# Spreading a layernorm's deviations over the partitions by selecting products, in the tail and for the first band

## The chip, the cores and the metric

The kernel runs on one core of one Trainium2 chip. The metric is the device time of an execution in microseconds (us); the median of several runs is given. The core has five engines that work side by side: TensorE (PE, with its weight loads PEld), VectorE (DVE), ScalarE (ACT), GpSimd (POOL) and SyncE (SP), and 16 DMA engines that all of them share. Here SP issues most transfers, ACT and POOL a few.

## The reference

The input x is (4, 128, 128, 128): four images of 128 channels and 128 x 128 pixels, float32. First comes a block with regional attention and a depthwise convolution, then two quantised 3x3 convolutions:

```python
reg = x[:, :, ih, iw]                      # regions of 16 x 16, step 14: 9 x 9 of them an image
tok = reg...reshape(b * n, rs * rs, c)
y = _ln(tok, ln1_g, ln1_b)                 # layernorm over the 128 channels
qkv = y @ w_qkv                            # 4 heads of 32
tok = softmax(q @ k.T * hd**-0.5) @ v @ w_out + b_out + tok
merged = out / cnt                         # regions added up where they overlap
y = _ln(xf, ln2_g, ln2_b) @ w_p0 + b_p0    # xf: merged, 128 channels; y: 256 channels
ym = depthwise 5x5 convolution of y
ym = gelu(batchnorm(ym)); y = gelu(ym) @ w_p2 + b_p2 + xf
...
# then: clip, 4-bit quantise, conv3x3, batchnorm, relu, quantise, conv3x3, batchnorm, add the identity
```

`_ln` takes the mean and the variance of a pixel over its 128 channels, and multiplies the centred pixel by one number, the inverse deviation `rsqrt(v + eps)`. This number is what the change is about.

## The kernel before

Channels lie on the 128 partitions and pixels along the free axis, so the sums of a layernorm run over partitions. The kernel doesn't centre: the weights that follow are multiplied by a centring matrix once, at the start. It needs only the inverse deviation of every pixel, on every partition.

The work goes by bands. A band is 16 rows of an image, the step is 14, so an image has NR = 9 bands and the four have T = 36. A band is cut into two blocks of up to LB = 8 rows, that is 1024 pixels. For each block `normalise` makes five steps:

- `squares`: ACT squares the block.
- `variance`: eight products on PE, with a column block of ones, 32 wide. The pixels are taken in four quarters of w = n / 4 = 256; the sums of quarter q are written to the 32 partitions from 32 q on, so each number stands on 32 partitions. ACT and DVE make the variance from two such sums (L364 to L368).
- `deviation`: ACT takes logarithm and exponential (L372, L373), which gives the tile `rstd` (128 x 256). Then ACT's queue stores one partition in 32 of it, four rows of 256, to a small tensor `row` in DRAM (L375).
- `spread`: SP's queue loads `row` back into a tile `xn` (128 x 1024), the four rows side by side, the same on all 128 partitions (L380).
- `scaled`: DVE multiplies the block by it in two halves, in place in `xn` (L389).

`ln1_chunks` uses this for the first layernorm, with the projections to queries and keys after it (L459, results copied by ACT); `post_chunks` for the second, with the products by w_out ahead of it (L511, L512) and the projection to 256 channels after it (`p0`, L527; ACT adds the bias, L532, and SP stores y to `y2_d` in DRAM). All products go through one pool of PSUM tiles, `pm`, with three buffers; the scores of the attention have their own.

The order of PE, ACT, DVE and SP is written out by hand, POOL's follows from the program too. For band 0 the first layernorm's steps run alone, the two blocks step by step (`for steps in zip(*ln1_chunks(0))`). Then, in every band t, `beside(t)` gives the work that is put between the nine regions' attention: the first layernorm of band t + 1, the second of band t - 1, steps of the depthwise convolution of an image that is done. There a row of deviations is on its way while PE works on attention.

After the last band comes a tail. The pools of the bands (`xp`, `yp`, `up`, `cp`, the attention's) are closed, and two pools `late1`, `late2` are opened on their memory. Then:

- `run(left)`: the last projections of the band before the last; SP stores them.
- `conv_rest`: allots the input tiles `u0` to `u7` and the weight tiles `w0` to `w7` of the last depthwise unit (rows 96 to 127 of the last image), issues all weight loads on POOL (L552, sixteen of 240 KB), and on SP the early part of the input loads of the first `early` tiles: rows that were stored before, of the first of two row groups (L655, two of 144 KB a tile).
- `run(beside(T))`: the second layernorm of the last band, alone. `row`, `xn`, `p0`, stores of y.
- `rest()`: the input loads that are left, `late(k)`, four of them ahead of the steps and then one with each step; and eight steps of the convolution, each with 96 small products (L566, 192 PE records), two copies by ACT (L686), statistics by DVE (L690), and stores of the result, half on SP's queue, half on ACT's (L695).

`late(k)` fetches, for a tile with an early part, the rest of the rows; for a tile without, the whole tile in four loads (two of 256 KB, two of 64 KB).

After the tail the batchnorm statistics are gathered, then follow the gelu stage and the two quantised convolutions; the change doesn't touch them. A second, safe form of the kernel's first half is built too and runs only when a flag says that scores may be large; it doesn't run with these inputs.

DMAs of SP and ACT take one of eight completion counters in turn, and a DMA waits until the last one on its counter has landed.

Of the kernel before, what the change touches and what calls it, by code (L numbers as in the profile page):

```python
# [22 lines left out]
LB = 8  # L23
# [23 lines left out]
def layers(  # L47
# [29 lines left out]
    nc = tc.nc  # L77
# [32 lines left out]
    ident = const.tile([P, P], F32, name="ident")  # L110
# [22 lines left out]
    with (  # L133
# [21 lines left out]
        for w in (wqkv, wp0.rearrange("p h m -> p (h m)")):  # L155
            n = w.shape[1]
# [18 lines left out]
    with ExitStack() as actx:  # L175
# [21 lines left out]
        xb, xr, yr, qs, kr, ob = {}, {}, {}, {}, {}, {}  # L197

        def scratch(n):

            return up.tile([P, 32 * CW], F32, name="u")[:, :n]
# [137 lines left out]

            return [load, largest, spread, clip_all, widen, to_int, to_f8]  # L340

        def normalise(src, n):

            held = {}
            w = n // 4

            def squares():  # L350
                held["sq"] = sq = work.tile([P, LB * P], F32, name="sq")
                nc.scalar.activation(sq[:, :n], src(), AF.Square)

            def variance():
                ps = ps_m.tile([P, 2, 256], F32, name="pm")
                for m, v in enumerate((src(), held.pop("sq"))):
                    for q in range(4):
                        nc.tensor.matmul(  # L358
                            ps[32 * q : 32 * q + 32, m, :w], ones, v[:, q * w : (q + 1) * w],
                            start=True, stop=True,  # L360
                        )
                held["rstd"] = rstd = dev.tile([P, 256], F32, name="rstd")
                rstd = rstd[:, :w]
                nc.scalar.activation(rstd, ps[:, 0, :w], AF.Square, scale=1.0 / P)  # L364
                nc.vector.scalar_tensor_tensor(
                    rstd, ps[:, 1, :w], 1.0 / P, rstd, ALU.mult, ALU.subtract
                )
                nc.vector.tensor_scalar(rstd, rstd, 0.0, None, ALU.max)  # L368

            def deviation():  # L370
                rstd = held.pop("rstd")[:, :w]
                nc.scalar.activation(rstd, rstd, AF.Ln, bias=eps_t)  # L372
                nc.scalar.activation(rstd, rstd, AF.Exp, scale=-0.5)  # L373
                held["row"] = row = rowp.tile([4, 256], F32, name="row")
                nc.scalar.dma_start(out=row[:, :w], in_=rstd[0:P:32, :])  # L375

            def spread():
                row = held.pop("row")
                held["xn"] = xn = xnp.tile([P, LB * P], F32, name="xn")
                nc.sync.dma_start(  # L380
                    out=xn[:, :n].rearrange("p (q w) -> p q w", q=4),
                    in_=bass.AP(row.tensor, row.offset, [[0, P], [256, 4], [1, w]]),
                )

            def scaled():
                xn = held.pop("xn")
                halves = [xn[:, hh * n // 2 : (hh + 1) * n // 2] for hh in range(2)]
                for hh, t in enumerate(halves):
                    nc.vector.tensor_tensor(t, t, src()[:, hh * n // 2 : (hh + 1) * n // 2], ALU.mult)  # L389
                return halves  # L390

            return squares, variance, deviation, spread, scaled
# [44 lines left out]
                        held[t][:, :, 0:2, :], held[t - 1][:, :, RS - 2 :, :]  # L437
                    )

        def ln1_chunks(t):  # L440

            chunks = []
            for at, (r, n) in enumerate(row_blocks(t)):
                held = {}
                squares, variance, deviation, spread, scaled = normalise(lambda r=r, n=n: xb[t, r][:, : n * P], n * P)

                def second(r=r, n=n, at=at, held=held, scaled=scaled):
                    held["xn"] = scaled()
# [42 lines left out]

            xr[t, n] = load_rows(rp, "xr", t, *finished(t)[n])

        def post_chunks(t):


            b, i = bands[t]
# [1 line left out]
            for at, (r, n) in enumerate(finished(t)):  # L499
                held = {}  # L500
                squares, variance, deviation, spread, scaled = normalise(
                    lambda n=n, held=held: held["xf"][:, : n * P], n * P
                )

                def project(hh, r=r, n=n, at=at, held=held):
# [138 lines left out]
        def conv_rest(n, w_t, u_t, c_t):  # L644
# [1 line left out]


            b, g0, ng = units[n]
            early = 5
            at = GR + 2  # L650

            def load(k, a, z, g, m):
# [193 lines left out]
        def beside(t):  # L846
# [5 lines left out]
            two = post_chunks(t - 1) if t else []  # L852
            had = len(todo)
            if t >= 2:
                b, i = bands[t - 2]
# [11 lines left out]
            n = len(todo) // share[0] if fresh else -(-len(todo) // max(share[0], 1))  # L867
# [63 lines left out]
        ga2, be2 = vector(gamma2, "ga2"), vector(beta2, "be2")  # L931
        with nullcontext() if safe else tc.manual_schedule(engines=MANUAL):
            ln1_begin(0)
            for steps in zip(*ln1_chunks(0)):
                run(steps)
            last = None
            for t in range(T):
# [88 lines left out]
    with (  # L1026
# [14 lines left out]
        for m in range(2):  # L1041
# [3 lines left out]
            for h in range(2):  # L1045
# [3 lines left out]
                    start=True, stop=True,  # L1049
# [301 lines left out]
```

## Time and profile before

| | us |
|---|---|
| median of 3 runs | 3292.92 |
| lowest, highest | 3278.27, 3293.81 |
| the profiled execution | 3289.4 |
| its span | 3287.5 |

| engine | busy us | share |
|---|---|---|
| PE | 3089.1 | 94% |
| DVE | 2018.0 | 61% |
| ACT | 1989.9 | 61% |
| POOL | 836.3 | 25% |

Where the stages lie in the profiled execution: the first layernorm of band 0 from 9 to 34 us, the bands from there to 2229, the tail from 2229 to 2334, then the gelu stage and the convolutions.

How to read the views. The timeline has, for each row, the start and the length in us, the engine (SPq, ACTq: that engine's queue issues a DMA), the line, the operation, what is written and read, how many instructions were merged, and in brackets how long the engine was idle before and what released it. The row of a DMA issue shows the issue alone, not the transfer. A float32 product of 128 x 512 is two PE records. The windows view has one row a stretch: its length, the busy time of PE, PEld, DVE, ACT and POOL (number of instructions), the granted clock of TensorE as a share of the full one, the share of the 16 DMA engines that was busy, and GB/s. The waits view has who waited for whom, us in total, times, and the longest. In the DMA view a queue has its packets, MB and share of the 16 engines' time; q1 is SP's queue, q10 ACT's, q0 POOL's. An issue row has the KB of one DMA and the median us to its landing.

### The profile page before, as it was taken

To read this page: it belongs to the slowest core of one execution; us is meant where nothing else is said; L and a number is where in the kernel's file an instruction comes from. 1 tells how busy PE (TensorE), PEld (TensorE's weight loads), DVE (VectorE), ACT (ScalarE), POOL (GpSimd) and SP (SyncE) were. 2 spreads that over 40 slices of the span, in tenths; PEclk is the share of its full clock that TensorE was granted. 3 is DMA by queue.
4 is the path that set the end of the run, shared out by engine and by line. 5 is a ranking of instruction groups with operands and counts; after the bars stand their busy time and mean duration, and the time that the engine had idled before them with its cause. 6 is when DMAs were issued, how large, how long until landed. Compare 5 with 4: busy or idle time off the path is not lost.

```text
span 3287.5 us, 75680 instructions
## 1 busy us (share of the span) xinstructions
PE 3089.1 (94%) x30922; PEld 1540.7 (47%) x30922; DVE 2018.0 (61%) x3247; ACT 1989.9 (61%) x2654; POOL 836.3 (25%) x1058
## 2 busy tenths in 40 slices
PE   7999999999999999999999998884899999999998
PEld 3555554544444554444444444553544444444343
DVE  4877887676766667666655564442455555666543
ACT  5777776777777776777656564432477767433443
POOL 3444443333333333333222232211111111000000
PEclk8999999999999999999999998876699999999999
DMA  4555677898886788886888888757899999452398
GB/s 92 133 164 166 173 181 177 195 212 196 204 202 163 192 208 204 195 208 166 190 200 207 202 195 201 192 160 186 256 356 358 358 358 300 150 167 70 101 359 308
DMA packets 810450, 682.75 MB, mean 208 GB/s; under 512 B 581014, under 2 KB 696047, under 8 KB 810095
## 3 DMA queue, kind: packets, MB, share of 16 engines
q1 hardware_dynamic: 799471, 671.26, 75.2%
q8 instruction: 246, 4.03, 0.5%
q0 software_dynamic: 1024, 3.93, 0.5%
q10 hardware_dynamic: 9600, 2.62, 0.4%
q14 instruction: 109, 0.89, 0.1%
HBM read 410.81 MB, written 270.81 MB: 207 GB/s over the span
## 4 chain that ended last, share of the span: by engine, by line
PE 76%; DMA 9%; ACT 5%; issue 4%; DVE 3%; SPq 2%; POOL 0%; ACTq 0%; DVEq 0%; POOLq 0%
PE pc L1125 19%; PE pm L566 9%; PE sc L749 9%; PE po L812 8%; PE pm L459 7%; PE pb L1183 6%; PE pm L527 5%; PE pm L735 4%; PE po L820 3%; DMA y_d<-y 3%; PE pm L358 3%; PE pm L511 3%; DMA u<-y_d 2%; ACT pt L757 1%; DMA xn<-row 1%
## 5 line engine op out<-in xcount | busy, mean ns | idle before, releaser
L832 DVE RECIPROCAL rd<-po 128x256 f32<-128x256 f32 x324 | 569.3, 1757 | 451.6 <-PE po L820 446.5
L1125 PE MATMUL pc<-q,wq 128*128 128x512 fp8e4 x3168 | 701.4, 381 | 14.3 <-DVE q L1137 14.3
L757 ACT ACTIVATE pt<-sc 128x1024 f32<-128x1024 f32 x648 | 627.8, 1024 | 129.1 <-PE sc L749 64.7
L767 POOL TENSOR_TENSOR sm<-pt 128x512 f32<-128x512 f32 x324 | 412.6, 1274 | 1052.8 <-ACT pt L757 748.8
L1125 PEld LDWEIGHTS <-wq 128*128 128x128 fp8e4 x3168 | 308.9, 98 | 417.2 <-issue 49.5
L749 PE MATMUL sc<-q,kr 32*128 32x256 f32 x5184 | 403.6, 414 | 18.9 <-ACT pt L757 18.8
L566 PE MATMUL pm<-u,w 40*32 40x504 f32 (+5 forms) x7680 | 369.2, 504 | 37.2 <-DMA u<-y_d 24.9
L749 PEld LDWEIGHTS sc<-q,kr 32*128 32x128 f32 x5184 | 249.1, 190 | 258.4 <-issue 166.4
L812 PE MATMUL po<-pt,v 128*32 128x256 f32 x5184 | 360.1, 397 | 7.8 <-DVE part L836 7.0
L527 PE MATMUL pm<-xn,wp 128*128 128x512 f32 (+1 forms) x576 | 251.9, 568 | 57.6 <-DVE xn L389 29.4
L613 ACT COPY c<-pm 128x512 f32<-128x512 f32 (+1 forms) x256 | 132.2, 562 | 269.1 <-PE pm L566 257.6
L532 ACT ACTIVATE y<-pm,bp 128x512 f32<-128x512 f32 (+1 forms) x288 | 182.9, 640 | 165.9 <-DMA y_d<-y 86.9
L459 PE MATMUL pm<-xn,wqkv 128*128 128x512 f32 (+1 forms) x576 | 251.9, 566 | 11.2 <-DVE xn L389 7.7
L767 DVE TENSOR_TENSOR sm<-pt 128x512 f32<-128x512 f32 x324 | 243.3, 751 | 27.4 <-ACT pt L757 27.4
L566 PEld LDWEIGHTS pm<-u,w 40*32 40x32 f32 x7680 | 147.0, 112 | 218.7 <-issue 163.5
L617 DVE BATCH_NORM_STATS2 st<-c 128x6 f32<-128x512 f32 (+2 forms) x320 | 160.8, 550 | 138.5 <-ACT c L613 137.9
L1183 PE MATMUL pb<-cv,wp 128*128 128x512 f32 x512 | 231.6, 596 | 6.8 <-ACT cv L1174 6.8
L812 PEld LDWEIGHTS po<-pt,v 128*32 128x32 f32 x5184 | 139.4, 111 | 181.2 <-issue 107.5
L1133 DVE BATCH_NORM_STATS2 st<-pc 128x6 f32<-128x512 f32 x256 | 165.6, 689 | 66.8 <-PE pc L1125 66.8
L820 PE MATMUL po<-sm,ones 128*32 128x256 f32 x2592 | 205.7, 388 | 0.0
L735 PE MATMUL pm<-wqkv,yr 128*128 128x128 f32 x1296 | 193.0, 290 | 0.0
L735 PEld LDWEIGHTS pm<-wqkv,yr 128*128 128x128 f32 x1296 | 158.7, 191 | 68.0 <-issue 44.3
(149 smaller groups left out, 3424.9 us busy)
## 6 DMA issues: line engine op xcount, KB each, us to landing
cv<-cv_d SPq DMA_DIRECT2D x64, 1024.0 KB
u<-y_d SPq DMA_DIRECT2D x230, 256.0 KB
cv_d<-c SPq DMA_DIRECT2D x192, 256.0 KB
xn<-row SPq DMA_DIRECT2D x80, 512.0 KB
y_d<-y SPq DMA_DIRECT2D x160, 256.0 KB
xfl<-xf_d SPq DMA_DIRECT2D x64, 512.0 KB
id_d<-y SPq DMA_DIRECT2D x64, 512.0 KB
idt<-id_d SPq DMA_DIRECT2D x64, 512.0 KB
```

The lines of the kernel that those rows point to most:

```text
L459: nc.tensor.matmul(pm[:, : n * P], wqkv[:, m * P : (m + 1) * P], held["xn"][hh], start=True, stop=True,)
L527: nc.tensor.matmul(pm[:, : n * P], wp0[:, h, :], held["xn"][hh], start=True, stop=True)
L566: nc.tensor.matmul(outs[half][32 * q : 32 * q + 32, j, :, a:z], wt[hs, s, c, :], ut[hs, :, c, a + s - 1 : z + s - 1], start=(s == 1), stop ...
L735: nc.tensor.matmul(pv[:, m, c, :], region(yr, j + m)[:, c * P : (c + 1) * P], wqkv[:, 2 * P :], start=True, stop=True,)
L749: nc.tensor.matmul(sc[h // 2][:, h % 2, kc, :].rearrange("p (r c) -> p r c", c=RS), region(kr, j)[hs, kc * P : (kc + 1) * P], queries(j, h ...
L757: nc.scalar.activation(pt, sc[p], AF.Exp)
L767: add(sm, pt[:, :, 0, :], pt[:, :, 1, :], ALU.add)
L812: nc.tensor.matmul(po[hs, 0, :], v[:, kc, hs], pt[h // 2][:, h % 2, kc, :], start=(kc == 0), stop=(kc == 1),)
L820: nc.tensor.matmul(po[hs, 1, :], ones, sm[h // 2][:, h % 2, :], start=True, stop=True)
L832: nc.vector.reciprocal(rd, po[:, 1, :])
L1125: nc.tensor.matmul(pc[:, h], w[:, t, :], q1[b][:, r + dy : r + dy + RB, dx : dx + P], start=(t == 0), stop=(t == 8),)
L1183: nc.tensor.matmul(pb[:, m], wp2[:, h, :], cv[:, h, px], start=(h == 0), stop=(h == 1))
```

## The change

`normalise` gets a third argument, a selecting matrix `sel`. Where it is given, the row store and the load of `xn` are left out. Instead PE spreads the deviations: the selector's column block q has ones on partition 32 q and zeros elsewhere, so its product with `rstd` (K = 128, 256 columns) writes row 32 q of `rstd` to all 128 partitions of PSUM. Four products make the block, into two `pm` tiles, and DVE's multiplication reads its factor from there. The selector is made by one copy on DVE from the identity, with each of its columns 0, 32, 64 and 96 repeated 128 times.

It is given in two places: for band 0's first layernorm, where it lies in a scratch tile, and for the tail's second layernorm, where it is allotted in the pool `late1` after the tiles of `conv_rest`. All other bands go through DRAM as before. And `early` in `conv_rest` is 3, not 5: four of the ten early loads are gone, and tiles 3 and 4 are fetched whole by `late`.

```diff
+        def selector(room):
+            sel = room[:, : 4 * P].rearrange("p (q m) -> p q m", m=P)
+            firsts = ident[:, 0:P:32]
+            nc.vector.tensor_copy(
+                sel, bass.AP(firsts.tensor, firsts.offset, [firsts.ap[0], firsts.ap[1], [0, P]])
+            )
+            return sel
+
-        def normalise(src, n):
+        def normalise(src, n, sel=None):
...
                 nc.scalar.activation(rstd, rstd, AF.Exp, scale=-0.5)
+                if sel is not None:
+                    held["rstd"] = rstd
+                    return
                 held["row"] = row = rowp.tile([4, 256], F32, name="row")
...
             def spread():
+                if sel is not None:
+                    rstd = held.pop("rstd")
+                    held["all"] = [ps_m.tile([P, 2, n // 4], F32, name="pm") for _ in range(2)]
+                    for q in range(4):
+                        nc.tensor.matmul(
+                            held["all"][q // 2][:, q % 2], sel[:, q], rstd, start=True, stop=True
+                        )
+                    held["xn"] = xnp.tile([P, LB * P], F32, name="xn")
+                    return
...
-                    nc.vector.tensor_tensor(t, t, src()[:, hh * n // 2 : (hh + 1) * n // 2], ALU.mult)
+                    by = held["all"][hh].rearrange("p q w -> p (q w)") if sel is not None else t
+                    nc.vector.tensor_tensor(t, by, src()[:, hh * n // 2 : (hh + 1) * n // 2], ALU.mult)
...
-            early = 5
+            early = 3
...
             ln1_begin(0)
-            for steps in zip(*ln1_chunks(0)):
+            sel = selector(scratch(4 * P))
+            for steps in zip(*ln1_chunks(0, sel)):
                 run(steps)
...
-            run(beside(T))
+            run(beside(T, selector(pools[0].tile([P, 4 * P], F32, name="sel"))))
             flush(len(stores))
             rest()
```

`ln1_chunks`, `post_chunks` and `beside` hand the selector on.

More of the change, by code (lines that the diff above doesn't have):

```diff
@@ L438, in ln1_begin, with ln1_chunks @@
                     )
-        def ln1_chunks(t):
+        def ln1_chunks(t, sel=None):
             chunks = []
@@ L444, in ln1_chunks @@
                 held = {}
-                squares, variance, deviation, spread, scaled = normalise(lambda r=r, n=n: xb[t, r][:, : n * P], n * P)
+                squares, variance, deviation, spread, scaled = normalise(
+                    lambda r=r, n=n: xb[t, r][:, : n * P], n * P, sel
+                )
                 def second(r=r, n=n, at=at, held=held, scaled=scaled):
@@ L492, in fetch, with post_chunks @@
             xr[t, n] = load_rows(rp, "xr", t, *finished(t)[n])
-        def post_chunks(t):
+        def post_chunks(t, sel=None):
             b, i = bands[t]
@@ L501, in post_chunks @@
                 squares, variance, deviation, spread, scaled = normalise(
-                    lambda n=n, held=held: held["xf"][:, : n * P], n * P
+                    lambda n=n, held=held: held["xf"][:, : n * P], n * P, sel
                 )
@@ L844, in attention, with beside @@
             return scores, halves, values_in, values
-        def beside(t):
+        def beside(t, sel=None):
             one = list(early) if t else ln1_chunks(1)
             early[:] = ln1_chunks(t + 2) if t + 2 < T else []
-            two = post_chunks(t - 1) if t else []
+            two = post_chunks(t - 1, sel) if t else []
             had = len(todo)
```

## The prediction

> **What bounds the kernel now.** I read the page first, for the shares; then the timeline around 16 and around 2250 us, the two places that the change touches; then the windows and the DMA view there.
>
> ```profile
> PE 3089.1 (94%) x30922; PEld 1540.7 (47%) x30922; DVE 2018.0 (61%) x3247; ACT 1989.9 (61%) x2654; POOL 836.3 (25%) x1058
> ```
>
> TensorE is busy for 94% of the span, so over most of it only fewer products, or a shorter wait of PE, can save time. The two stretches concerned are exceptions: PE stands still. First the start:
>
> ```profile
> 16.11 1.05 ACTq L375 DMA_DIRECT2D row<-rstd  x1
> 17.78 3.57 SPq L380 DMA_DIRECT2D xn<-row  x2
> 21.65 1.29 DVE L389 TENSOR_TENSOR xn<-xn,xt 128x512 f32<-128x512 f32 x2 [5.69 <-DMA xn<-row]
> 22.40 2.08 PE L459 MATMUL pm<-xn,wqkv 128*128 128x512 f32 x2 [7.67 <-DVE xn L389]
> 25.42 8.35 PE L459 MATMUL pm<-xn,wqkv 128*128 128x512 f32 x14 [0.94 <-ACT q L466]
> 33.70 1.51 PE L749 MATMUL sc<-q,kr 32*128 32x256 f32 x16
> ```
>
> The deviations are ready at 16.09 and the first scaled half leaves VectorE at 22.3: two transfers, one after the other, lie between. PE waits 7.67 us. Then the tail:
>
> ```profile
> 2236.39 12.40 SPq L655 DMA_DIRECT2D u<-y_d  x10
> 2239.37 0.48 ACTq L375 DMA_DIRECT2D row<-rstd  x1
> 2251.68 2.21 SPq L380 DMA_DIRECT2D xn<-row  x2
> 2266.71 2.54 DVE L389 TENSOR_TENSOR xn<-xn,xf 128x512 f32<-128x512 f32 x4 [27.43 <-DMA xn<-row]
> 2267.46 9.48 PE L527 MATMUL pm<-xn,wp 128*128 128x512 f32 x16 [29.41 <-DVE xn L389]
> 2270.28 8.49 SPq L399 DMA_DIRECT2D y_d<-y  x8
> 2280.97 14.63 SPq L655 DMA_DIRECT2D u<-y_d  x16
> 2285.28 15.50 PE L566 MATMUL sc<-u,w 40*32 40x128 f32 x534 [8.35 <-DMA u<-y_d]
> ```
>
> One chain sets the end here: row out, row back into 128 partitions (landed 2266.7), projection, stores of y, and only then the late loads of u that read those stores, and the convolution. But what is the chain waiting in?
>
> ```profile
> SPq L655 <- DMA row<-rstd: 8.5, 1, 8.5
> q0 software_dynamic: 1024, 3.93, 46.4%
> q1 hardware_dynamic: 1698, 3.73, 39.0%
> w<-dw_d POOLq DMA_DIRECT2D x14, 240.0 KB, 13.4
> 2264.00:2268.00 4.00, 0.54 (x1) 0.50 (x2) 1.29 (x3) 0.00 (x0) 0.00 (x0) 0.50 0.54 218
> 2268.00:2272.00 4.00, 4.00 (x6) 1.47 (x5) 1.25 (x3) 1.37 (x2) 0.00 (x0) 0.50 0.21 43
> ```
>
> The first line is from the waits of SP's queue; the queue lines are for 2236 to 2268: the 16 DMA engines are 85% occupied, by the weights that POOL fetches (q0) and SP's traffic (q1). SP's seventh load of u waited 8.5 us because its completion counter was shared with the tiny row store, and SP's later issues queued behind it. So the wait is not latency of an idle system: most of it is a full DMA system, and only the last two windows (DMA share 0.54 and 0.21) show DMA idle because the chain has nothing to send.
>
> [...]q0 and q1 both move in this window, so removing SP traffic helps POOL's weights and the other way round, and the sum of engine time decides. [...]the products of L459 are 0.85 us apart at first and 0.43 us from 30.2 on, and the granted clock is 0.50 from 16 to 28. [...]the trace has 0.69 us for L389 from SBUF, and 0.83 for L512 (another operation, from PSUM). I take 0.7.
>
> **The change, part by part.** A 128x512 product is two PE records, so a 128x256 spreading product costs 2 x 0.215 = 0.43 us at full clock and 0.86 at half.
>
> *Start.* Removed: two row stores (ACT, 1.05 and 0.49 of issue) and two loads of xn (SP). Added: one selector copy, and eight products. The copy (128x512) isn't in the trace; the nearest rows are VectorE's scalar operations of 128x1024 (L1201, 0.69) and of 128x384 (L152, 0.42), so about 0.5, bounds 0.3 and 1.0. VectorE is idle from 8.3 to 9.84 and hides it. The first four products can start at 16.2, cold: to 19.64. The second four: [...]warm, to 21.35; if not, to 23.1. The eight projections follow at 0.86 each warm (PE is the slowest: ACT needs 0.69), so to 28.3 or 30.0, against 33.77. VectorE scales the first half at 18.1 while PE goes on, and the three pm buffers are free in time (one product waits for a half that is scaled at 18.9, before its turn). ACT's last copy of kr then frees the second scores products at 29.1 or 30.7 against 34.50. Gain 5.4 or 3.8; I take 4.7. SP's loads of the next band move forward with VectorE and stay hidden.
>
> *Tail, compute.* The selector is drawn from the late pool, over memory just closed, so (the built program's waits show it) VectorE's copy waits for the last stores of cv_d, as POOL's first weight load did until 2234.2. It stands ahead of the four L512 operations, which began at 2232.42, and can hold them, and with them xf and both deviations, for 1 to 2.4 us; I take 1.5. Then deviation at 2240.9, eight warm products 3.5 us, and eight projections 6.9 us, of which the second chunk's spreading goes ahead: last y at about 2252.5, against 2278.0. By compute alone that is 25 us earlier.
>
> *Tail, transfers.* That is not what can be had. Before the late loads may start, the engines must still move: weights, 46.4% of 32 us = 14.8; six early loads instead of ten (0.88 MB) and two stores of xf (1.05 MB) at 39.0% x 32 / 3.73 = 3.35 us per MB, 6.5; and eight stores of y, 2.10 MB, of which 1.57 took 95% of the 8 us from 2272, so 10.2. Sum 31.5 us from 2236. At full occupation that ends at 2267.5; with 85% for the first 21.3 and 95% for the rest, at 2271.8. I take 2270 against 2280.97: 11 us. The 1.5 us of the selector's wait is hidden by this: y is ready 15 us before the engines are through with it.
>
> *Later.* Four 144 KB loads of tiles 3 and 4 become parts of late loads, 0.59 MB. SP's late loads of tile 3 have from 2281 to 2302 before, of tile 4 from 2301 to 2309, and DMA is occupied to 0.30 and 0.33 in the windows 2288 to 2296; so they fit. But the eight steps of L566 take 49.0 us, 42 of them at their own pitch (5.3), and the stalls (largest 1.73 and 1.21) stand where DMA is full: 1 us more, bounds 0 and 5. PE is cold there in either kernel (granted 0.50 throughout)[...].
>
> Sum: 4.7 + 11 - 1 = 14.7. The profiled execution took 3289.4 (span 3287.5), so 3275. The median of the timed runs, 3292.92, lies 3.5 above it, their lowest, 3278.27, lies 11 below: the profile stands in the middle of the spread, and I leave the sum there. Half a per cent, about what a measurement of this kernel can tell from no change, is 16.5 us of the median, so the border is 3276.5: the forecast sits on it.
>
> **Rivals.**
> 1. Transfers give most of it back. The weights' 6 KB pieces hold up the small pieces of y, the late loads begin at 2273.5 (gain 7.5), and the fuller late loads stall steps 3 and 4 by 4 us. For: DMA is full to 2263. Against: q0 and q1 shared evenly. 3289.4 - 4.7 - 7.5 + 4 = 3281.
> 2. The tail gains more. With the row gone SP is never blocked, the engines fill to the last gap and y overlaps the weights: late loads at 2267, no added stall, the better start: 14 + 5.4, 3270. For: SP stood still for 8.5 us. Against: the weights kept the engines busy meanwhile.
> 3. Slower. SP's late loads of a step are queued behind the stores of an earlier step. If tiles 3 to 7, now all loaded whole, each arrive after their step could begin, each of five steps waits for 655 KB at 0.18 MB/us, 3.6, plus a store's landing, about 3.5: 7 us each, 35 in all. 3289.4 - 15.7 + 35 = 3309. It decides from 3 us a step. Against: before, tiles 5 to 7 were loaded whole and their steps show stalls of at most 1.2 us.
> 4. The deviations don't arrive sooner because the selector waits for something later than the stores of cv_d: only the start gains, 3285. The pool's other tile, w, was filled from 2234, which speaks against it.
>
> **How the numbers follow.** Forecast 0.50 (own range 3269 to 3281), rival 1 0.22, rival 2 0.20, rival 3 0.04, rival 4 0.04. The range to 8 in 10 takes in rivals 1, 2 and 4 and leaves out 3, with a few us either way for the spread of the runs: 3262 to 3287. Faster by over 0.5%: 0.6 of the forecast, all of rival 2 and a little of rival 1, 0.55; slower only by rival 3 and chance, 0.04; the same 0.41.
>
> **What would show it.** In the profile after: projections of the first band done by 28 to 30; no row of rstd at 16 or 2240; VectorE's copy of the selector in the tail ending near 2234 in the old count; last y 15 us or more before DMA is through with the stores; late loads 9 to 13 us after nothing but DMA (share 0.85 or more between); eight steps of L566 in 49 to 52 us. Wrong would be: late loads starting within 5 us of the old place, steps at even pitch of 8 us or more, or a change outside these two stretches.

## The result and the profile after

| | before | after |
|---|---|---|
| median | 3292.82 us (6 runs, 3278.27 to 3297.27) | 3273.77 us (6 runs, 3271.47 to 3283.68) |
| the profiled execution | 3289.4 us, span 3287.5 | 3272.91 us, span 3271.1 |

The ratio is 0.9946, 95% interval 0.9926 to 0.9967. A later comparison on another chip gave 0.9948 (0.9934 to 0.9961). The forecast was 3275 us, 14.7 below the profiled execution of before; that of after is 16.5 below it. As differences of mean times the two comparisons give 14.4 ± 7.0 and 14.6 ± 4.9 us, together 14.6 ± 4.0. (Here and below ± is twice the standard error of a difference of means, each against runs of before on the same chip.) The two ratios themselves, times the mean of before, make 17.8 and 17.1 us: how the runs are averaged moves the figure by 3 us, which is less than its uncertainty, and the forecast lies in both intervals.

The first row of the page's first section:

```profile
PE 3100.5 (95%) x30954; PEld 1550.6 (47%) x30954; DVE 2019.6 (62%) x3249; ACT 1990.9 (61%) x2654; POOL 837.5 (26%) x1058
```

PE is as busy as before, and its share rises to 95%. The start in the timeline of after (line numbers have moved, L483 is the old L459, L773 the old L749):

```profile
16.28 3.72 PE L394 MATMUL pm<-rstd,u 128*128 128x256 f32 x16 [1.41 <-ACT rstd L382]
17.45 0.69 DVE L411 TENSOR_TENSOR xn<-pm,xt 128x512 f32<-128x512 f32 x1 [1.34 <-PE pm L394]
...
19.83 7.03 PE L483 MATMUL pm<-xn,wqkv 128*128 128x512 f32 x16
...
26.79 1.51 PE L773 MATMUL sc<-q,kr 32*128 32x256 f32 x16
```

The spreading products follow the deviations at once, and the projections follow them with no gap (no brackets in the row of L483). They take 7.03 us, not 11.4: the records are 0.43 us apart from the first on. The scores begin at 26.79 against 33.70, 6.9 us sooner. Now the tail:

```profile
2221.66 0.43 DVE L346 COPY sel<-ident 128x512 f32<-128x512 f32 x1 [3.68 <-DMA cv_d<-c]
2222.00 2.72 DVE L536 SCALAR_TENSOR_TENSOR xf<-pm,bo,xr 128x512 f32<-128x512 f32 x4
2224.83 2.81 SPq L679 DMA_DIRECT2D u<-y_d  x6
2228.62 5.41 PE L394 MATMUL pm<-rstd,sel 128*128 128x256 f32 x16 [1.35 <-ACT rstd L382]
2233.86 6.17 PE L551 MATMUL pm<-xn,wp 128*128 128x512 f32 x14
2235.64 22.24 SPq L421 DMA_DIRECT2D y_d<-y  x8
2253.90 0.69 ACT L556 ACTIVATE y<-pm,bp 128x512 f32<-128x512 f32 x1 [15.72 <-DMA y_d<-y]
2260.05 7.69 SPq L679 DMA_DIRECT2D u<-y_d  x14
2264.24 0.65 PE L590 MATMUL sc<-u,w 40*32 40x128 f32 x8 [7.53 <-DMA u<-y_d]
```

The last reciprocal of the bands (DVE, attention of the last region) begins at 2215.70, 11.1 us sooner than before. Counted from it, the late loads begin at +44.35 us instead of +54.16. The row and both loads of xn are gone. But a wait has come that the forecast doesn't have: ACT's fifth y waits 15.72 us for a store of the first block's y, because each half of the 256 channels has only two tiles for y (`y2t`), and the third must wait until the store of the first has landed. PE's last projection stands behind it. The windows of the same stretch (columns as in the section on the profile):

```profile
2222.00:2230.00 8.00, 5.58 (x42) 2.33 (x41) 4.21 (x10) 4.48 (x8) 5.11 (x10) 0.95 0.98 199
2230.00:2238.00 8.00, 8.00 (x23) 5.05 (x22) 2.77 (x4) 2.56 (x4) 2.26 (x5) 0.84 0.91 212
2238.00:2246.00 8.00, 2.04 (x5) 0.57 (x3) 0.00 (x0) 0.19 (x1) 1.12 (x3) 0.80 0.84 213
2246.00:2254.00 8.00, 0.00 (x0) 0.00 (x0) 0.00 (x0) 0.10 (x1) 0.00 (x0) 0.50 0.84 272
2254.00:2260.00 6.00, 2.08 (x2) 0.50 (x2) 0.00 (x0) 2.65 (x4) 0.00 (x0) 0.50 1.05 218
```

The engines stand still for most of the time from 2240 to 2254, and the DMA share stays at 0.84 or more. Two readings are open: the y tiles cost time, or they only wait beside transfers that have to be done anyway.

### The profile page after: what moved, and what is told of

It reads as the page before. It is cut to its first block, busy times and chain, and to the rows that moved or that the text cites. A ratio compares the mean times of both kernels' runs of the same rounds, so it can differ in the third digit from the quotient of the medians.

```text
span 3271.1 us, 75716 instructions
## 1 busy us (share of the span) xinstructions
PE 3100.5 (95%) x30954; PEld 1550.6 (47%) x30954; DVE 2019.6 (62%) x3249; ACT 1990.9 (61%) x2654; POOL 837.5 (26%) x1058
## 3 DMA queue, kind: packets, MB, share of 16 engines
q0 software_dynamic: 1024, 3.93, 0.5%
## 4 chain that ended last, share of the span: by engine, by line
PE 79%; DMA 7%; ACT 4%; issue 4%; DVE 3%; SPq 2%; POOL 0%; ACTq 0%; DVEq 0%; POOLq 0%
PE pc L1150 19%; PE pm L590 9%; PE sc L773 9%; PE po L836 8%; PE pb L1208 7%; PE pm L483 7%; PE pm L551 5%; PE pm L759 4%; PE po L844 4%; PE pm L367 3%; PE pm L535 3%; DMA y_d<-y 2%; ACT pt L781 1%; DMA u<-y_d 1%; DMA xn<-row 1%
## 5 line engine op out<-in xcount | busy, mean ns | idle before, releaser
L781 ACT ACTIVATE pt<-sc 128x1024 f32<-128x1024 f32 x648 | 628.1, 1024 | 133.6 <-PE sc L773 69.1
L1150 PEld LDWEIGHTS <-wq 128*128 128x128 fp8e4 x3168 | 309.1, 98 | 417.7 <-issue 50.3
L773 PE MATMUL sc<-q,kr 32*128 32x256 f32 x5184 | 404.6, 415 | 18.5 <-ACT pt L781 18.3
L773 PEld LDWEIGHTS sc<-q,kr 32*128 32x128 f32 x5184 | 250.0, 191 | 258.6 <-issue 166.9
L551 PE MATMUL pm<-xn,wp 128*128 128x512 f32 (+1 forms) x576 | 249.7, 564 | 36.4 <-ACT y L556 35.6
L791 DVE TENSOR_TENSOR sm<-pt 128x512 f32<-128x512 f32 x324 | 243.6, 752 | 25.7 <-ACT pt L781 25.7
L483 PE MATMUL pm<-xn,wqkv 128*128 128x512 f32 (+1 forms) x576 | 248.5, 560 | 2.7 <-ACT v L764 2.0
L759 PEld LDWEIGHTS pm<-wqkv,yr 128*128 128x128 f32 x1296 | 158.7, 191 | 69.9 <-issue 44.4
```

Of the source, the lines that this page charges most:

```text
L483: nc.tensor.matmul(pm[:, : n * P], wqkv[:, m * P : (m + 1) * P], held["xn"][hh], start=True, stop=True,)
L551: nc.tensor.matmul(pm[:, : n * P], wp0[:, h, :], held["xn"][hh], start=True, stop=True)
L759: nc.tensor.matmul(pv[:, m, c, :], region(yr, j + m)[:, c * P : (c + 1) * P], wqkv[:, 2 * P :], start=True, stop=True,)
L773: nc.tensor.matmul(sc[h // 2][:, h % 2, kc, :].rearrange("p (r c) -> p r c", c=RS), region(kr, j)[hs, kc * P : (kc + 1) * P], queries(j, h ...
L781: nc.scalar.activation(pt, sc[p], AF.Exp)
L791: add(sm, pt[:, :, 0, :], pt[:, :, 1, :], ALU.add)
```

## The experiments

Landmarks (moments that every trace has, so that kernels can be compared at them), from one profiled execution of each kernel: the first scores product; then, counted from the start of the last reciprocal of the bands, DVE's first xf (L536) and the first late load of u; then the eight depthwise steps from first to last product; the span.

| kernel | scores | xf | late loads | steps | span | mean time against before |
|---|---|---|---|---|---|---|
| before | 33.70 | +5.61 | +54.16 | 49.0 | 3287.5 | |
| after | 26.79 | +6.30 | +44.35 | 51.3 | 3271.1 | -14.4 ± 7.0 |
| after_again | 28.30 | +6.13 | +43.27 | 48.9 | 3273.7 | -14.6 ± 4.9 |
| start_only | 28.46 | +5.62 | +57.65 | 49.4 | 3281.3 | -3.0 ± 3.7 |
| start_again | 28.21 | +5.62 | +57.14 | 48.4 | 3276.8 | -1.9 ± 3.1 |
| tail_only | 33.53 | +7.20 | +41.61 | 51.1 | 3269.9 | -12.7 ± 3.4 |
| all_early5 | 26.96 | +6.65 | +49.51 | 50.6 | 3272.1 | -11.8 ± 2.9 |
| early3_only | 34.60 | +5.61 | +52.95 | 50.3 | 3288.7 | -2.7 ± 3.6 |
| ytail | 26.94 | +8.33 | +45.94 | 48.2 | 3261.9 | -15.3 ± 4.5 |
| weights_late | 26.14 | +8.78 | +39.42 | 59.8 | 3261.7 | -17.7 ± 3.5 |
| pool_late | 26.37 | +8.24 | +44.61 | 48.9 | 3262.1 | -11.5 ± 2.8 |
| pool_late_y | 26.75 | +6.50 | +42.53 | 49.1 | 3271.1 | -11.5 ± 3.1 |
| warm_start | 32.01 | +5.61 | +55.99 | 49.9 | 3273.8 | +2.4 ± 3.5 |
| warm8 | 31.77 | +5.62 | +57.79 | 51.0 | 3281.1 | one run |

Spans of single executions don't rank kernels: runs of before on one chip lie between 3273.94 and 3299.69. Landmarks within a stage repeat within 2 to 4 us in most traces.

**The two halves of the change alone** (start_only, tail_only), each the changed kernel with the other place as before; then start_only once more:

```diff
# start_only
-            early = 3
+            early = 5
-            run(beside(T, selector(pools[0].tile([P, 4 * P], F32, name="sel"))))
+            run(beside(T))
# tail_only
-            sel = selector(scratch(4 * P))
-            for steps in zip(*ln1_chunks(0, sel)):
+            for steps in zip(*ln1_chunks(0)):
```

> The changed kernel with its edits for the first band alone; the tail and the early loads as before. Theory A (the start gives what the two traces differ by there, and keeps it): first scores product at 26.5 to 27.5 us, span 6 to 7 us shorter than before, late loads of u as far after the last band as before (65.3 us after its last reciprocal). Theory B (the forecast's term, 4.7): scores at 28 to 30. Rival C (the start's gain is lost or changed in the bands that follow, because loads or clock stretches meet other work): scores at 27, but the last band's reciprocal less than 3 or more than 10 us earlier than before.

> The changed kernel with its edits in the tail alone (selector there, and three tiles with early loads); the first band as before. Theory A: counted from the last band's last reciprocal, late loads of u start 9 to 11 us sooner than before, the eight depthwise steps take 51 us, so the end comes 7 to 9 us sooner; first scores at 33.7. Rival C: the tail's gain depends on where the bands left it, then under 5 or over 13. The sum test: gains of this kernel and of the one with the start alone add up to that of the whole change (16.4 us of span) within 3 us if nothing else acts; a rest of 4 us or more lies in the bands between.

> The changed kernel's edits for the first band alone, once more, for the size of its effect on the time. Theory A (the start's 6 to 7 us reach the end): mean 4 to 7 us under before. Rival B (the bands take it back, their clock's dips come sooner): mean 0 to 2 us under before. First scores at 26 to 28.5 in either.

The ratios are 0.9995 (0.998 to 1.001), 0.9961 (0.9948 to 0.9973) and, for the repeat, 0.9986 (0.9972 to 1.0). The tail alone carries nearly all: 12.7 us of 14.6. The two comparisons of the start give 2.4 ± 2.4 us together, less than the 5 to 6 us by which the first scores of these two traces come sooner. What was expected came only in part. The scores of start_only, 28.46, lie in the range of B and not of A. Its 65.3 us is a slip, taken across two traces (2280.97 less 2215.70); within the trace of before it is 54.16. The late loads of tail_only come 12.6 us sooner than in the trace of before, and 14.9 sooner than the mean of five traces with the old tail: more than A said, and by the second count C's over 13. In mean times the two parts make 15.7 us, so nothing is missing from the whole; their spans, 6.2 and 17.6 us shorter against 16.4, miss it by 7.4, which differences of single executions can do. In the traces the gain is still there hundreds of microseconds later: the first reciprocal of band 10 comes at 532.0, 530.9 and 533.2 in the three kernels with the old start and no fillers (before, tail_only, early3_only), and 5.6 to 9.6 us before 532.0 in the nine with the selector. From there to the last reciprocal both kinds take alike: 1689 to 1695 us in those three, 1680 to 1698 in the nine (means 1692 and 1689). So the bands don't visibly take it back, and the spread between executions, 18 us there, hides the rest. Of the repeat's two theories the time is nearer B (1.9 us), the traces speak for A. C of start_only asked for more than 10 us at the last reciprocal, and the two traces have 11.4 and 14.1; but warm_start, with the old start, has 16.3, so this landmark can't decide.

**The unaltered kernel again.**

> The changed kernel once more, unaltered: how far its landmarks repeat. Expected: scores at 26.5 to 27.5 and the same waits in the tail within 1 us each, late loads 44 to 46 us after the last band's last reciprocal; but the last reciprocal anywhere from 2211 to 2221, because the granted clock's dips lie elsewhere. If instead the reciprocal comes back within 1 us of 2215.7, the drift in the bands belongs to the program and not to the execution. The ratio to before is expected at 0.9945 to 0.9965.

The waits repeat (ACT's fifth y 16.9 us with its neighbours, against 16.2). The other landmarks lie outside what was expected: scores at 28.30, late loads at +43.27, the last reciprocal at 2224.26, not 2215.70. So the 11.1 us by which the bands ended sooner in the first pair are in part an accident of the execution, and so are 1.5 us of the 6.9 at the scores (what differs there is told under the clock, below). The steps took 48.9 us, not 51.3: the first pair's +2.3 was an accident too.

**Early loads: five tiles or three.** all_early5 is the changed kernel with `early = 5`; early3_only is before with `early = 3`.

> The changed kernel with five tiles that have early loads, as before, instead of three. Theory A (forecast's transfer sum): 0.59 MB more ahead of the late loads at 3.35 us per MB, so late loads start 2 us later than in the changed kernel, the steps take 49 to 50 us instead of 51.3, and the time is within 2 us of it. Rival B (the early loads stand in the way of the chain): late loads 4 us later or more, time 3 us longer. Rival C (fewer early loads only stall the steps): late loads at the same place, steps 2 us shorter, time 2 us shorter than the changed kernel.

> The kernel before with three tiles that have early loads instead of five, deviations through DRAM as before. Theory A (the wait of SP's queue is part of a full DMA system): four loads fewer move the landing of the deviations' row by 2 us, late loads 2 us sooner, steps 1 to 2 us longer, time the same within 2 us. Rival B (the blocked issue on SP is what cost): SP's seventh load, which stood 8.5 us on the row store's counter, is gone, so the load of xn is issued 5 to 9 us sooner and late loads start 5 to 9 us sooner, which would be most of the tail's gain without any selecting product.

Ratios 0.9967 (0.9954 to 0.998) and 0.9992 (0.998 to 1.0005). The late loads of all_early5 fit its rival B: +49.51, 5 to 6 us behind the two traces of the changed kernel and 8 behind tail_only, which has the same tail. The 3 us of time that B adds are neither shown nor refuted (11.8 ± 2.9 us under before, the changed kernel 14.6 ± 4.0). The timeline of all_early5 shows a blocked queue:

```profile
2222.81 13.52 SPq L679 DMA_DIRECT2D u<-y_d  x10
2232.87 0.69 ACT L556 ACTIVATE y<-pm,bp 128x512 f32<-128x512 f32 x1 [5.38 <-PE pm L551]
2238.53 2.88 SPq L421 DMA_DIRECT2D xf_d<-xf  x2
2243.11 17.52 SPq L421 DMA_DIRECT2D y_d<-y  x8
```

And in the waits of its SP queue (us in total, times, longest):

```profile
SPq L679 <- DMA u<-y_d: 9.4, 2, 7.0
```

The ninth and the tenth load wait, 9.4 us, for the counters of the first two, and the stores of xf and y stand behind them. The first y is ready at 2233.56 and its store is issued at 2243.11; in after it goes at once (2234.92 + 0.69, issue at 2235.64). But after's queue waits for loads of u as well, with two of its stores. Six loads and two stores of xf are issued without such a wait; the ninth transfer and the tenth, stores of y, wait 6.4 and 1.1 us:

```profile
SPq L421 <- DMA u<-y_d: 7.5, 2, 6.4
```

What the block alone costs isn't shown. From xf to the late loads all_early5 takes 42.8 us, after 38.0. Of the 4.8 us, 2.3 are engine time of SP's queue (50.7% of 42.8 us against 51.1% of 38.0), near the 2 us that A has for the 0.59 MB; 1.2 are engine time of the same weights, and 1.3 time in which the engines stand idle. How much of these last two is the blocked queue, and how much the spread between executions, stays open.

In early3_only the row still goes through DRAM: its late loads come at +52.95, 1.2 us before those of the profile of before and 3.6 before the mean, 56.5, of the five traces with the old tail (before, start_only twice, the two with fillers below). It doesn't test B, because the block didn't go. It moved from a load of u to the store of xf:

```profile
SPq L421 <- DMA row<-rstd: 8.4, 1, 8.4
```

That fewer early loads alone bring most of the tail's gain is refuted all the same, since the tail alone, which adds the products, lies at +41.61. The time of early3_only, 2.7 ± 3.6 less, isn't told from none.

**More tiles for y** (ytail): two more for each half, in the tail alone.

```diff
+            free = xnp.tile([P, LB * P], F32, name="xn")
+            for h in range(2):
+                y2t[h].append(pools[0].tile([P, RB, 2, CW], F32, name=f"y3_{h}"))
+                y2t[h].append(free[:, 512 * h : 512 * h + 512].rearrange("p (r e x) -> p r e x", r=RB, e=2))
```

> The changed kernel with two more tiles for y in each half, in the tail alone, so that the second block's y need not wait for the stores of the first. Theory A (the DMA engines are full, the tile wait only stands beside that): ACT's fifth y no longer waits 15 us, last y about 11 us sooner, but the late loads of u only 0 to 4 us sooner, time 0 to 4 us less than the changed kernel. Rival B (the tile wait is a term of its own that the forecast overlooked): late loads 8 us sooner or more, 36 us after the last reciprocal instead of 44.4, time 8 us less.

The timeline of ytail:

```profile
2228.10 7.03 PE L551 MATMUL pm<-xn,wp 128*128 128x512 f32 x16
2235.16 0.69 ACT L556 ACTIVATE xn<-pm,bp 128x512 f32<-128x512 f32 x1 [0.17 <-PE pm L551]
2255.53 6.19 SPq L679 DMA_DIRECT2D u<-y_d  x12
```

And its windows:

```profile
2234.00:2242.00 8.00, 1.13 (x3) 0.19 (x1) 0.00 (x0) 1.51 (x3) 1.01 (x2) 0.89 0.84 241
2242.00:2250.00 8.00, 0.00 (x0) 0.00 (x0) 0.00 (x0) 0.00 (x0) 0.00 (x0) 0.50 0.84 254
2250.00:2256.00 6.00, 0.00 (x0) 0.00 (x0) 0.00 (x0) 0.00 (x0) 0.00 (x0) 0.50 1.02 217
```

The last y is done at 2235.85, 26.3 us after the last reciprocal, where after has 41.7. The late loads don't move: +45.94 against +44.35 and +43.27. Counted from xf it is 37.6 us against 38.0 and 37.1. The DMA shares are the same, with the compute engines idle. Against the changed kernel on the same chip the mean is 0.7 ± 5.9 us lower; ratio to before 0.9954 (0.994 to 0.9968). Theory A: the 15.7 us wait, the longest of the stretch, costs nothing that the landmarks show, though they would not show 2 or 3 us. The DMA view of ytail says what y waits for instead. These are POOL's queue and SP's from 2236 to 2240, and SP's from 2248 to 2252:

```profile
q0 software_dynamic: 135, 0.53, 50.6%
q1 hardware_dynamic: 110, 0.33, 33.6%
q1 hardware_dynamic: 3001, 0.76, 89.1%
```

The stores of y move in small packets: 253 B on average in the last line (0.76 MB in 3001), 252 B in the trace of before from 2272 to 2280 (1.57 MB in 6238), where nothing else moved. The first of them is issued at 2231.15, after six loads of u (from 2220.74) and two stores of xf (2223.15). Yet from 2236 to 2240, beside POOL's weights, SP's queue moved only 110 packets, of 3 KB on average, so hardly any of y's; from 2248 to 2252 the small ones take 89.1% of the engines' time. In six traces with the selector and three early tiles (all but weights_late) the late loads begin 7.1 to 7.9 us after the last packet of these weights, whatever the engines waited for before.

**Half of the weights later** (weights_late): the loads for tiles 4 to 7 go from POOL to SP's queue, behind the late loads of tiles 0 to 3.

```diff
-            for k in range(NCK):
+            for k in range(NCK // 2):
                 weights(W[k], k, 0, 2, nc.gpsimd.dma_start)
...
                 for k in range(4):
                     late(k)
+                for k in range(NCK // 2, NCK):
+                    weights(W[k], k, 0, 2, nc.sync.dma_start)
```

> The changed kernel with the depthwise weights of tiles 4 to 7 (eight loads of 240 KB) issued by SP's queue behind the late loads of tiles 0 to 3 instead of by POOL ahead of them. Theory A (the sum of engine time ahead of the late loads decides): half of the weights' 14.8 us leaves the stretch, so late loads start 6 to 8 us sooner, 37 to 38.5 us after the last reciprocal; the steps grow by 1 to 3 us; time 4 to 6 us less than the changed kernel. Rival B (a wait decides, for y's tiles or for compute): late loads less than 3 us sooner, and the time same or longer because the steps wait for weights. Rival C (steps stall): late loads sooner, but steps 6 us longer or more, no gain.

Counted from the last reciprocal, as the expectation did, the late loads come 4 to 5 us sooner than in the two traces of the changed kernel: less than A's 6 to 8, more than B's 3. Counted from xf, which came late here (+8.78), the stretch is 30.6 us, against 38.0, 37.1, 37.6 and 34.4 in the four traces with this tail (ytail among them) and all weights ahead: 4 to 7 us shorter. So fewer bytes do shorten the stretch; that it is by the whole of the sum isn't shown. Then the steps of rival C:

```profile
2257.89 8.45 SPq L576 DMA_DIRECT2D w<-dw_d  x8
2266.44 0.93 SPq L719 DMA_DIRECT2D cv_d<-c  x2
2277.40 1.07 ACT L710 COPY c<-sc 128x512 f32<-128x512 f32 x2 [18.17 <-DMA cv_d<-c]
2280.24 3.59 PE L590 MATMUL sc<-u,w 40*32 40x128 f32 x117 [9.17 <-DMA cv_d<-c]
```

The weights stand ahead of SP's stores of the result; ACT waits 18.2 us for one such store to free a tile `c`, and PE's wait of 9.2 us is put down to the same kind of store. The steps take 59.8 us. Ratio 0.9945 (0.9931 to 0.9959); against the changed kernel on the same chip the mean is 3.1 ± 5.2 us lower, which decides nothing.

**The same on POOL's queue** (pool_late), with a copy ahead that reads a late row of tile 0, and with the extra y tiles (pool_late_y):

```diff
+                gate = small.tile([P, 1], F32, name="gate")
+                nc.gpsimd.tensor_copy(gate[:32], U[0][:32, 1, 0, 0:1])
+                for k in range(NCK // 2, NCK):
+                    weights(W[k], k, 0, 2, nc.gpsimd.dma_start)
```

> The changed kernel with the weights of tiles 4 to 7 behind the late loads, but on POOL's queue: a copy of 32 x 1 on POOL that reads a late row of tile 0 stands ahead of these eight loads, so they start when the first late load has landed and block nothing on SP. Theory A (weights behind SP's stores, not the weights themselves, made the steps of the kernel with late weights on SP 59.8 us long): late loads 36 to 40 us after the last reciprocal as there, steps 49 to 53 us without a wait of PE for a store of the result, time 4 to 7 us less than the changed kernel. Rival B (the weights simply don't fit beside the steps): steps 57 us or more, PE waits for w at the fifth step, no gain over the changed kernel.

> The kernel with late weights on POOL, and two more tiles for y in each half in the tail. Theory A (engine time decides, the y tiles stand beside it): late loads within 2 us of the kernel without the extra tiles, time the same. Theory A2 (with half of the weights gone the engines have gaps, and now the wait for y's tiles, 7.6 us where the late weights were on SP, comes into the path): late loads 3 to 6 us sooner than without the tiles, 32 to 36 us after the last reciprocal, time 3 to 6 us less.

Neither kernel did what it was meant to. POOL's order isn't written by hand, nothing ties the loads to the copy, and in POOL's timeline fourteen of the sixteen loads stand ahead of it:

```profile
2231.40 0.51 POOL L576 DMA_DIRECT2D w<-dw_d  x1 [1.68 <-DMA w<-dw_d]
2255.02 0.18 POOL L732 COPY gate<-u 32x1 f32<-32x1 f32 x1 [23.12 <-DMA u<-y_d]
2255.25 1.00 POOL L576 DMA_DIRECT2D w<-dw_d  x2
```

So they are the changed kernel with two weight loads later, and behave nearly like it: from xf to the late loads 36.4 and 36.0 us, ratios 0.9964 (0.9951 to 0.9977) and 0.997 (0.9957 to 0.9982). They repeat that extra y tiles bring nothing that can be seen, here 0.4 us of the stretch and 0.0 ± 3.3 us of the time. Whether late weights that block nobody would win stays open.

**The clock in the start** (warm_start): the kernel before with twelve unread products in the gap of PE; then with eight (warm8).

```diff
+                if n == 2 and not safe:
+                    idle = ps_s.tile([P, 2, 2, NT], F32, name="sc0")
+                    for m in range(12):
+                        nc.tensor.matmul(
+                            idle[:, m % 2].rearrange("p a n -> p (a n)"), ident, xb[0, 0][:, :512],
+                            start=True, stop=True,
+                        )
```

> The kernel before with twelve products added that nobody reads (identity by rows of x, 128 x 512, into a tile of the scores), in the gap of 16 to 22 us in which PE waits for the first band's deviations through DRAM. Theory A (a good part of the start's gain is that PE doesn't stand still and its clock stays up): the first scaled half arrives as before at 22.3, but the eight projections take 7 to 8 us instead of 11.4, scores at 29.5 to 30.5 instead of 33.7, that is half to two thirds of the change's 6.9 us without any selector. Rival B (the gain is the wait alone): scores at 33 or later, the fillers only push the projections back.

> The kernel before with eight unread products in the start's gap instead of twelve (twelve took 10.6 us, 0.43 a record, and pushed the projections from 22.0 to 25.0). Theory A (clock): the projections start at 22.0, their sixteen records take 7 to 8 us, scores at 29 to 30, 4 to 5 us of the change's 6.9. Rival B (the wait alone): scores at 32.5 or later.

Warm8's timeline:

```profile
14.79 7.13 PE L939 MATMUL sc<-xt,ident 128*128 128x512 f32 x16
22.30 1.12 PE L459 MATMUL pm<-xn,wqkv 128*128 128x512 f32 x2 [0.39 <-DVE xn L389]
24.65 1.29 DVE L389 TENSOR_TENSOR xn<-xn,xt 128x512 f32<-128x512 f32 x2 [1.80 <-DMA xn<-row]
25.59 6.25 PE L459 MATMUL pm<-xn,wqkv 128*128 128x512 f32 x14 [2.16 <-DVE xn L389]
31.77 1.51 PE L749 MATMUL sc<-q,kr 32*128 32x256 f32 x16
```

With the fillers the granted clock is 1.00 in all windows from 16 to 34, in both kernels, and back to back the records are 0.43 us apart. Yet the scores come only 1.9 us sooner, and 1.7 in warm_start: later than either theory A (29 to 30.5), sooner than either rival B. After one projection PE waits 2.16 us for the second block, whose row lands at about 24.6. In the kernel before the slow products covered most of this (PE's wait after its first projection is 0.94 there). So with the transfers kept, the full clock brings about 1.9 of the 6.9 us; the other 5.0 need the loads gone. The time of warm_start isn't less: ratio 1.0008 (0.9997 to 1.002).

With the loads gone the clock still varies from one execution to the next. The spreading products of start_only, behind the same pause of PE as in after:

```profile
16.26 5.41 PE L394 MATMUL pm<-rstd,u 128*128 128x256 f32 x16 [1.41 <-ACT rstd L382]
```

They take 5.41 us, not 3.72. The windows from 16 to 20 us have a granted clock of 0.65 here, 0.57 in after_again and 0.58 in start_again, and of 1.00 in the other six kernels with the selector. The scores follow: 28.2 to 28.5 in the three, 26.1 to 27.0 in the six.

## Why the prediction was right

*The sum.* 14.7 forecast, 14.6 ± 4.0 measured. That the two agree so closely is in part luck. In the landmarks every term came out better than forecast: the start 6.7 for 4.7, the transfers of the tail 13.5 for 11, the steps 0 for -1, together 20.2. The time shows 14.6 of it, and what is missing lies mainly at the start, with 2.4 ± 2.4 in the time. The mechanism in the tail was right, and most of the gain is there.

*Start, 4.7.* Sized too small. With the selector the scores begin at 26.1 to 28.5 in nine traces, mean 27.2; with the old start at 33.9, mean of three: 6.7. The forecast let the first four spreading products run cold, to 19.64, and the second four perhaps warm, to 21.35; when the clock would rise was the author's estimate. Three traces do this or nearly this: in after_again the projections begin at 21.34 and the second scores products at 29.10, where the forecast has 29.1. The other six have a case that the forecast left out, the full clock from the first product on. The pause of PE ahead of them doesn't decide it, for it is 1.36 to 1.41 us in all nine (with the old start it was 7.67 in the trace of before). What decides it isn't shown. In windows of 0.2 us the granted clock of before falls to 0.50 at 16.0 and is back at 1.00 at 29.7; that of after stays at 1.00 until it falls at 37.8, and is back at 41.2. In start_only the mean is 0.65 over the 4 us from 16 and 0.92 over the next 4. What the runs don't confirm is the full 6.7 in the time: 2.4 ± 2.4. Why it is less isn't settled. One reading of the lines was wrong without harm: the 0.83 us for L512 is the pitch of four that follow PE's products (3.33 us in all), each of them took 0.75; the multiplication from PSUM (L411) took 0.69, as long as L389's from SBUF.

*Tail, transfers, 11.* Right in kind and slightly small: the late loads stand at 54.2 to 57.8 us after the last reciprocal in five traces with the old tail, mean 56.5, and at 41.6 to 44.4 in three with the new one, mean 43.1. That transfers decide, and not the engines' waits, is shown by ytail and weights_late together. From xf to the late loads, in us (engine time is the stretch times its DMA share in the windows, a rough measure: single windows above go up to 1.05):

| | stretch | DMA share | engine time |
|---|---|---|---|
| before, 2232.4 to 2281 | 48.6 | 0.83 | 40.3 |
| after, 2222 to 2260 | 38.0 | 0.92 | 35.0 |
| all_early5, 2220 to 2262.8 | 42.8 | 0.90 | 38.5 |
| ytail, 2218 to 2255.5 | 37.5 | 0.91 | 34.1 |
| tail_only, 2227.3 to 2261.7 | 34.4 | 0.93 | 32.0 |
| weights_late, 2212 to 2242.4 | 30.4 | 0.91 | 27.7 |

After saves 5.3 us of engine time and 5.3 us of idle time of the engines (8.3 less 3.0). The first is fewer bytes on SP's queue, 4.53 MB for 6.39, of which two broadcast loads of xn (128 x 1024 float32 each) make 1.05 and the early loads 0.59. Tail_only, whose tail is that of after, shows how far executions differ: 3.6 us of stretch, and 3.0 of engine time for the same bytes. In all five tails with the selector the engines are busy for 0.90 to 0.93 of the stretch, whatever the compute engines wait for meanwhile. That less traffic of SP helps POOL's weights was the author's estimate, from two queues that move in one window, and isn't shown: the median landing of a weight load is 13.0 us in before and 13.1 in after (the DMA views of these stretches).

*Early loads, 0.59 MB at 3.35, inside that term: 2.0.* Undone in the changed kernel the edit costs 5 to 8 us of late-load time, of which 2.3 us are SP's engine time, as forecast. For the rest the forecast has no term. It didn't see that with the row gone a queue of ten early loads still blocks, for 9.4 us at the ninth and tenth, where before had 8.5 us on the row's counter. That this block is the missing term is likely but not shown.

*Tail, compute: last y by 2252.5 in the old count, 25 us sooner.* Wrong. The last y came 9.5 us sooner, counted from the last reciprocal (+41.74 against +51.19), because of the two y tiles for each half. With more tiles it comes at +26.3 in ytail, close to the forecast's +25.7. (The eight spreading products took 5.41 us in after, not 3.5: the clock was partly at half, 0.65 on average from 2228 to 2232.) It didn't matter to the late loads, as ytail shows: the path was the transfers, as the prediction held. The test that the prediction gave itself, last y 15 us ahead of the end of the transfers, therefore failed (the late loads came 2.6 us after it).

*The selector's wait, 1.5, bounds 1 to 2.4.* xf moved from +5.61 to +6.1 to +8.8 in eight traces: 0.5 to 3.2, mean 1.7. The value holds, the bounds were too narrow. Rival 4 is out: the copy ended at 2222.09, 6.4 after the last reciprocal.

*Steps, +1.* Nothing: the mean is 49.7 us in six traces with five early tiles and 49.7 in seven with three, weights_late left out. Rival 3, which needed 3 us for each of several steps, is out; its 3.5 us for the landing of a store was an estimate, and the three stores of cv_d on the chain of before that ended last took 3.7 to 5.2 us. Rival 1 is out by its numbers: the late loads came sooner than it says, and the steps didn't stall more. Its picture of y's small pieces held up beside the weights (whose packets are 3.8 KB, 3.93 MB in 1024, not 6) is what the DMA view of ytail shows, but the forecast's sum counts the same bytes ahead of the late loads. Rival 2's late loads, 14 us sooner, fit the means (13.5) better than the forecast's 11; its time, 3270, lies 3.8 from the median, the forecast's 1.2, which is less than the time's own uncertainty.

## What to carry to other kernels

Where the DMA system is full ahead of a dependent load, as here with shares of 0.90 to 0.93, count the bytes ahead of it: 1.97 MB of weights fewer shortened the stretch by 4 to 7 us. The longest wait of an engine in such a stretch may cost nothing: more tiles took away one of 15.7 us and brought 0.7 ± 5.9. Count also how many transfers a queue issues before the one that matters: with ten early loads the ninth waited 7.0 us, and all behind it waited too. A gain of 6 us at the start of a kernel whose runs spread by 25 us has to be shown in landmarks and in many runs, and the two need not agree.

## What the runs showed of the hardware

In the steps of after PE pauses at about every 128th depthwise product, each with a weight load of its own. Its timeline:

```profile
2289.21 3.86 PE L590 MATMUL sc<-u,w 40*32 40x126 f32 x127 [0.66 <-issue]
2293.53 3.63 PE L590 MATMUL sc<-u,w 40*32 40x126 f32 x126 [0.46 <-issue]
2298.34 3.62 PE L590 MATMUL sc<-u,w 40*32 40x128 f32 x128 [1.17 <-issue]
```

"issue" means that PE waited for nothing that the profile shows. From 2282 to 2304 there are five such pauses of 0.4 to 1.2 us, 3.4 us in all. A queue of kind instruction moved 0.18 MB in 11 packets between 2264 and 2316; whether the pauses have to do with it isn't shown, no run isolates their cause.

The granted clock is 0.50 all through the steps of before (2285 to 2335), though PE is busy for 44.28 of these 50 us, and 0.50 in after from 2260 to 2316, with PE busy for 45.01 of 56.

DVE's copy of the selector, 128 x 512 with each of four columns repeated 128 times, took 0.43 us.
